# A sequence of four layers on one core: three edits to its last stage (who adds k's rotations, when GEGLU's tokens are transposed, and a drain written out step by step)

## The chip, the core and the metric

One core of a Trainium2 chip runs one program. Its engines work side by side, each through its own queue in order: TensorE (PE, with weight loads shown as PEld), VectorE (DVE), ScalarE (ACT), GpSimd (POOL) and SyncE (SP), which here only issues DMAs. The metric is the device time of one execution in microseconds (us); lower is better. For the kernel before, three runs took 1828.2, 1832.02 and 1840.76 us, a median of 1832.02.

## The reference, cut to what matters

The input is x, 8 batches of 512 tokens of 128 channels, float32. Four layers follow, each with a residual sum and a layer norm. Only the fourth is touched by the change; it is two rounds of local attention and a gated MLP:

```python
def _layer(x, wqkv, qs, ksc, wo, lg, lb, w1, b1, w2, b2):
    h = shift_token(x)                      # half of the channels come from the token before
    q, k, v = split(h @ wqkv)               # 8 heads of 64
    q = l2norm(q) * qs;  k = l2norm(k) * ksc
    q, k = rotary_xpos(q, k)                # q*cos + rotate_half(q)*sin, the same for k
    o = local_attention(q, k, v)            # windows of 64, each sees itself and the one before
    x = x + o @ wo
    h = layernorm(shift_token(x)) * lg + lb
    a, g = split(h @ w1 + b1)               # 341 columns each
    return x + (a * gelu(g)) @ w2 + b2
for l in range(2):
    x = _layer(x, wqkv[l], ...)
out = layernorm(x_in + x)
```

## The kernel before, in words

The four layers run one after the other. The fourth is `ffn1` (its loop is called the last stage here); its three first chunks are begun by `early`, inside the attention before it, and the rest is `main`. Work is cut into 16 *items* k (round l = k // 8, batch k % 8) of four *chunks* c of 128 tokens, 64 chunks in all (`LAST`). The loop at line 986 runs over steps t. Every step issues a bit of several chunks at different depths, in an order written out by hand, and every call is kept in program order (line 629), so that order is each engine's queue.

What step t issues, with c = t % 4, and the names the profile shows for it:

- `begin` (chunk t): the products `q_ps` and `k_ps`. `squares` (ACT) and `rotate` (DVE, lines 705 to 710) read them. `rotate` leaves two products for q (n = 0) and for k (n = 1): with the cosine in `r` (shown as `was_k`), with the sine in `t2` (shown as `was_q`).
- `sizes` (line 715): DVE reduces the squares by head (`was_v<-was_k`), POOL adds `t2` to `r` for q and k in one operation of 128x1024 (`was_k<-was_k,was_q`). `norms` (line 721), on POOL: a maximum, a power (`was_v<-was_v`, 128x16), and k times its reciprocal norm (`was_k<-was_k,was_v`, 128x512).
- `operands_T` (chunk t-1): PE transposes k's half of `r`, then q's (`t_ps`); ACT copies them (`kT`, `qT`).
- `scores`, `maxima`, `weights` (chunk t-2): PE puts the mask and the scores in `sp`; DVE takes maxima and scales them in `m<-m,was_v`; ACT makes eight exponentials `pw`. `over_sums` (t-3) divides them on POOL (`pw<-pw,den`). `weights_T`, `weights_taken`, `values`, `values_taken` (t-4): PE `p_ps`, DVE `pT`, PE `o_ps`, ACT `oT`.
- `sums` (t-5 for attention, t-11 for the MLP): PE `y_ps`, DVE adds to `xs`.
- Once per item, two items back: at c = 0, after `sums`, four DMAs load the shifted tokens `hn`. At c = 1 `normed` takes moments (DVE `bn`, `st`; POOL `rstd`, `mr`) and adds b2 and x to `xs` on POOL; ACT normalizes `hn` as the last thing but `sums`. At c = 2, after `maxima`, `geglu` (line 954) transposes `hn` (`nT`), ACT copies it, and three times PE makes `gp` and `ap`, ACT the Gelu `u`, DVE the product. In the second round a finished batch has its moments taken at c = 2 (`moments(.., "f")`), and at c = 3 `finished` (line 965) normalizes it on ACT (`xn`) and sends it out.

PSUM: `q_ps`, `k_ps` and the two `sp` tiles have one bank each; everything else takes turns in four banks (`bank`). The steps past t = `LAST` begin no chunk; they drain what is under way: the last four chunks' attention, the GEGLU of items 14 and 15, their sums, and the last three layer norms.

Of the kernel before, what the change touches and what calls it, by code (L numbers as in the profile page):

```python
# [9 lines left out]
F32 = mybir.dt.float32  # L10
# [3 lines left out]
AF = mybir.ActivationFunctionType  # L14
ALU = mybir.AluOpType
# [3 lines left out]
P = 128  # L19
B, S, D = 8, 512, 128  # L20
NT = S // P
# [13 lines left out]
HID = 341  # L35
H_CH = [(0, 128), (128, 128), (256, 85)]
# [15 lines left out]
def body(ctx, tc, x, consts, rows, wa0, wa1, acols, bo, wf, wqkv, wo, w1, w2, cols, b2r, qs, ks, out):  # L52
# [6 lines left out]
    xs = outer.tile([P, B * NT, D], F32, name="xs")  # L59
# [9 lines left out]
    w1_s = outer.tile([P, 2, 2 * HID], F32, name="w1_s")  # L69
    w2_s = outer.tile([P, 2, 3, D], F32, name="w2_s")  # L70
    cols_s = outer.tile([P, 2, 8], F32, name="cols_s")
# [11 lines left out]
    half = outer.tile([P, NT], F32, name="half")  # L83
    nc.vector.memset(half, -0.5)
    ident = cst[:, C_ID : C_ID + P]
# [539 lines left out]
    def ffn1():  # L625
# [4 lines left out]
        mm, tr, act, copy = kept(nc.tensor.matmul), kept(nc.tensor.transpose), kept(nc.scalar.activation), kept(nc.scalar.copy)  # L630
        v_tt, v_stt, v_max, v_copy = (
            kept(f) for f in (
                nc.vector.tensor_tensor, nc.vector.scalar_tensor_tensor, nc.vector.tensor_reduce, nc.vector.tensor_copy
            )
        )
        v_stats, v_aggr, v_inv = kept(nc.vector.bn_stats), kept(nc.vector.bn_aggr), kept(nc.vector.reciprocal)
        p_tt, p_ts, p_set = (
            kept(f) for f in (
                nc.gpsimd.tensor_tensor, nc.gpsimd.tensor_scalar, nc.gpsimd.memset
            )  # L640
        )
# [3 lines left out]
        PAD, K = 64, 2 * B  # L645
        LAST = NT * K
        item = [{} for _ in range(K)]
# [30 lines left out]
        def tables(l):  # L678
            for n in range(2):
                s = lambda a, z: sc[:, l, n, a:z].unsqueeze(1).broadcast_to([P, NT, z - a])  # L680
                for k, a, z, by in ((0, 0, 64, (0, 64)), (1, 0, 32, (32, 64)), (1, 32, 64, (0, 32))):
                    p_tt(tab[:, l, n, k, :, a:z], tab[:, l, n, k, :, a:z], s(*by), ALU.mult)

        def shifted(src, h):

            p_set(h[0:1, 0, 64:128], 0.0)
            for at, n in ((0, 112), (112, 15)):
                nc.sync.dma_start(out=h[at + 1 : at + 1 + n, :, 64:128], in_=src[at : at + n, :, 64:128])
            nc.sync.dma_start(out=h[0:1, 1:NT, 64:128], in_=src[P - 1 : P, 0 : NT - 1, 64:128])
            nc.sync.dma_start(out=h[:, :, 0:64], in_=src[:, :, 0:64])  # L690
            return h

        def rows_of(k):
            return slice((k % B) * NT, (k % B + 1) * NT)
# [20 lines left out]
        def sizes(k, c, h):  # L715
            ss = sss[(NT * k + c) % 2]
            v_max(ss, h.pop("sq").rearrange("p n (h d) -> p (n h) d", d=DH), AX.X, ALU.add)
            p_tt(h["r"], h["r"], h.pop("t2"), ALU.add)
            h["ss"] = ss

        def norms(k, c, h):
# [8 lines left out]
        def load(k):  # L730
            item[k]["h"] = shifted((xs if k >= B else xn)[:, rows_of(k), :], hq)
# [32 lines left out]
        def main():  # L764
            with ExitStack() as st:
# [3 lines left out]
                bank = lambda name: p_b.tile([P, S], F32, tag="b", name=name)  # L769
# [9 lines left out]
                for i in range(2):  # L779
                    t = const.tile([P, 4, PAD + S], F32, name=f"kT{i}")  # L780
                    nc.gpsimd.memset(t[:, :, 0:PAD], 0.0)
                    kTs.append(t)
                work = pool("w", 2)
# [14 lines left out]
                def transposed(src, name, bufs):  # L798
                    ps = bank(name)
                    for c in range(NT):  # L800
                        tr(ps[:, c * P : (c + 1) * P], src[:, c, :], ident)
                    t = work.tile([P, S], F32, tag=name, name=name, bufs=bufs)
                    copy(t, ps)
                    return t
# [137 lines left out]
                def normalized(x, dst, shape):  # L942
                    r, m = shape
                    for c in range(NT):
                        act(dst[:, c, :], x[:, c, :], AF.Identity, bias=m[:, c : c + 1], scale=r[:, c : c + 1])

                def normed(k):
                    l, x = k // B, xs[:, rows_of(k), :]
                    item[k]["shape"] = moments(item[k]["hn"], "h")
                    p_tt(x, x, b2[:, l, :].unsqueeze(1).broadcast_to([P, NT, D]), ALU.add)  # L950
                    if l:
                        p_tt(x, x, xn[:, rows_of(k), :], ALU.add)

                def geglu(k):
                    l, nT = k // B, transposed(item[k].pop("hn"), "nT", 1)
                    u = work.tile([P, 3, S], F32, tag="u", name="u", bufs=2)
                    for c, (at, n) in enumerate(H_CH):
                        gp, ap = bank("gp"), bank("ap")
                        for ps, o in ((gp, HID), (ap, 0)):
                            mm(ps[0:n], lhsT=w1_s[:, l, o + at : o + at + n], rhs=nT, start=True, stop=True)  # L960
                        act(u[0:n, c, :], gp[0:n], AF.Gelu, bias=cols_s[0:n, l, 3 + c : 4 + c])
                        v_stt(u[0:n, c, :], ap[0:n], cols_s[0:n, l, c : c + 1], u[0:n, c, :], ALU.add, ALU.mult)
                    item[k]["u"] = u

                def finished(b):
                    x = slice(b * NT, (b + 1) * NT)
                    normalized(xs[:, x, :], xn[:, x, :], item[B + b].pop("shape"))
                    nc.sync.dma_start(out=ov[:, b], in_=xn[:, x, :])
# [3 lines left out]
                def load_T(k):  # L972
                    item[k]["hT"] = transposed(item[k].pop("h"), "hT", 3)

                def at_(j, f, *a):
                    if 0 <= j < LAST:
                        f(*divmod(j, NT), chunk[j], *a)

                def begun(t, f, *a):
                    if t >= EARLY:  # L980
                        at_(t, f, *a)
# [1 line left out]
                def begin(k, c, h):  # L983
                    proj(k, c, h, [p_qk.tile([P, INNER], F32, tag=f"{n}", name=f"{n}_ps") for n in "qk"])

                for t in range(1, LAST + 11):
                    k, c = divmod(t, NT)
                    if c == 1 and k + 1 < K:
                        load(k + 1)
                    begun(t, begin)  # L990
                    at_(t - 4, weights_T)
                    begun(t, squares, 1)
                    begun(t, rotate, 0)
                    at_(t - 3, over_sums)
                    at_(t - 4, weights_taken)
                    at_(t - 2, scores)
                    begun(t, squares, 0)
                    at_(t - 2, maxima)
                    if c == 3 and k + 1 < K:
                        load_T(k + 1)  # L1000
                    if c == 2 and 0 <= k - 2 < K:
                        geglu(k - 2)
                    if c == 1 and 0 <= k - 2 < K:
                        normed(k - 2)
                    begun(t, rotate, 1)
                    at_(t - 2, v_of)
                    at_(t - 1, operands_T)
                    at_(t - 1, operands)
                    at_(t - 4, values)
                    begun(t, sizes)  # L1010
                    at_(t - 2, weights)
                    begun(t, norms)
                    at_(t - 4, values_taken)
                    if c == 1 and 0 <= k - 2 < K:
                        h = item[k - 2]["hn"]
                        normalized(h, h, item[k - 2].pop("shape"))
                    sums(t - 5, t - 11)
                    if c == 0 and 0 <= k - 2 < K:
                        hn = work.tile([P, NT, D], F32, tag="hn", name="hn", bufs=1)
                        item[k - 2]["hn"] = shifted(xs[:, rows_of(k - 2), :], hn)  # L1020
                    if t in (4, 5):
                        scaled_weights(t - 4)
                    if t == 6:
                        tables(1)
                    z = t - 11
                    if z >= B * NT and z % NT == NT - 1:
                        item[z // NT]["shape"] = moments(xs[:, rows_of(z // NT), :], "f")
                        if z == LAST - 1:
                            finished(B - 1)
                    if z > B * NT and z % NT == 0:  # L1030
                        finished(z // NT - 1 - B)

        return early, main

    with tc.tile_pool(name="ops", bufs=1) as ops:
# [50 lines left out]
        for i in range(2):  # L1086
            for j in range(2):
                nc.sync.dma_start(
                    out=ks_[i][64 * j + 32 : 64 * j + 48].bitcast(F32),
                    in_=rowq.bitcast(F32).unsqueeze(1).broadcast_to([16, 8, S]),  # L1090
                )
        last = ffn1()
        for _ in ffn0(qs_, ks_, va, second, lambda: attention(1, False, qs_, ks_, va, second, spare=last[0], alone=16)):
            pass
# [99 lines left out]
```

## Time and profile before

| | |
|---|---|
| median of three runs | 1832.02 us |
| the profiled execution | 1831.37 us, of which its span is 1829.6 us |
| busy over the span | PE 1652.3, DVE 1349.6, ACT 1257.1, POOL 945.1 us |
| last stage: `main` | from about 1087 us to the end |
| 1600 to 1700 us | PE 96.88, DVE 76.28, ACT 81.71, POOL 92.78 us, clock 1.00 |
| 1795 to 1802 us | PE 0.21 us, clock 0.69 |

The page gives the granted clock of PE as a share of full speed. In a timeline a row is: start, duration, engine, line, operation, what it writes <- what it reads, how often, and in square brackets the idle time of the engine before it and what ended that. Rows that follow each other closely are merged. All rows of the last stage have line 629, so operations are told apart by tile names.

### The profile page before, as it was taken

How to read it: one execution, taken by the hardware profiler on the slowest of the kernel's cores; microseconds unless marked ns; L12 is line 12 of the kernel's file. 1: busy time of each engine (PE TensorE's matmuls, PEld its weight loads, DVE VectorE, ACT ScalarE, POOL GpSimd, SP SyncE). 2: the span in 40 equal slices, each digit the busy share in tenths (PEclk: the TensorE clock that was granted, in tenths of full speed). 3: DMA queues.
4: the chain of work that ended last, by engine and by line, in shares of the span. 5: the costliest groups of instructions: out<-in, count | busy, mean ns of one | idle time of the engine just before them, and what ended most of it. 6: DMA issues, size and time to landing. Idle time of an engine off the chain costs nothing.

```text
span 1829.6 us, 41974 instructions
## 1 busy us (share of the span) xinstructions
PE 1652.3 (90%) x16292; PEld 952.5 (52%) x16293; DVE 1349.6 (74%) x2185; ACT 1257.1 (69%) x2992; POOL 945.1 (52%) x954
## 2 busy tenths in 40 slices
PE   1699999999977679999999988899999999999984
PEld 1345555455545544444444445566666666666653
DVE  2588778878848788888888947677777777777752
ACT  0277777777754437877778867777777777888872
POOL 3223322232124542323222268988888888999972
PEclk6699999999998889999999999999999999999997
DMA  6823222221110223332223101111111111111110
GB/s 114 210 65 69 57 52 60 55 65 25 14 13 1 49 61 79 71 70 54 60 64 60 42 1 36 30 38 39 35 33 38 34 37 35 42 39 39 33 33 24
DMA packets 92648, 90.25 MB, mean 49 GB/s; under 512 B 45937, under 2 KB 57969, under 8 KB 92450
## 3 DMA queue, kind: packets, MB, share of 16 engines
q1 hardware_dynamic: 87760, 86.57, 21.5%
q8 instruction: 129, 2.11, 0.5%
q0 software_dynamic: 4096, 0.54, 0.2%
q14 instruction: 69, 0.57, 0.1%
q10 hardware_dynamic: 594, 0.47, 0.1%
HBM read 41.85 MB, written 18.87 MB: 33 GB/s over the span
## 4 chain that ended last, share of the span: by engine, by line
PE 67%; POOL 12%; DVE 8%; ACT 7%; issue 2%; DMA 2%; SPq 1%; ACTq 0%; DVEq 0%; POOLq 0%
PE av L250 14%; PE s_ps L250 11%; PE t_ps L250 9%; POOL was_k L629 4%; POOL was_v L629 4%; PE y_ps L629 4%; PE sp L629 3%; PE gp L629 2%; PE o_ps L629 2%; ACT e L48 2%; PE ap L629 2%; PE o_ps L251 2%; PE t_ps L629 2%; PE q_ps L629 2%; PE k_ps L629 2%
## 5 line engine op out<-in xcount | busy, mean ns | idle before, releaser
L48 DVE TENSOR_REDUCE m<-s_ps 128x2 f32<-128x1024 f32 x512 | 621.4, 1224 | 171.4 <-PE s_ps L250 167.3
L48 ACT ACTIVATE e<-t_ps 128x512 f32<-128x512 f32 x1024 | 556.2, 596 | 183.5 <-PE t_ps L250 175.9
L250 PE MATMUL av<-e,va 128*32 128x256 f32 x4096 | 328.5, 393 | 10.8 <-ACT avs L48 10.7
L250 PE MATMUL s_ps<-k,q 63*128 63x512 f32 x1024 | 264.2, 511 | 31.7 <-DMA k<-far 23.0
L48 POOL DMA_DIRECT2D q<-mt x128 | 69.1, 543 | 368.8 <-ACT mt L48 368.7
L250 PE MATMUL t_ps<-q,k 64*128 64x512 f32 x1024 | 247.1, 447 | 1.3 <-ACT e L48 1.3
L629 ACT ACTIVATE pw<-sp,m,was_v 128x128 f32<-128x128 f32 x512 | 227.3, 475 | 0.9
L250 PEld LDWEIGHTS s_ps<-k,q 63*128 63x128 f32 x1024 | 99.1, 189 | 238.8 <-issue 160.0
L629 POOL TENSOR_TENSOR was_v<-was_v 128x16 f32<-128x16 f32 x64 | 187.7, 2933 | 5.3
L629 POOL TENSOR_TENSOR was_k<-was_k,was_q 128x1024 f32<-128x1024 f32 x64 | 151.1, 2361 | 61.8 <-DVE was_q L629 61.7
L250 PEld LDWEIGHTS av<-e,va 128*32 128x32 f32 x4096 | 81.8, 108 | 101.1 <-issue 59.2
L250 PEld LDWEIGHTS t_ps<-q,k 64*128 64x128 f32 x1024 | 122.0, 189 | 22.6 <-ACT e L48 10.6
L629 POOL TENSOR_TENSOR pw<-pw,den 128x1024 f32<-128x1024 f32 x64 | 121.3, 1896 | 7.6 <-DVE den L629 7.6
L629 ACT ACTIVATION_READ_ACCUMULATOR pw<-sp,m,was_v 128x1 f32 x512 | 113.3, 221 | 0.0
L250 PEld LDWEIGHTS <-sel 64*128 64x128 bf16 x2048 | 66.7, 97 | 75.8 <-issue 43.5
L629 DVE TENSOR_REDUCE m<-sp 128x4 f32<-128x512 f32 x128 | 82.5, 686 | 27.7 <-PE sp L629 25.8
L629 ACT COPY v<-v_ps 128x512 f32<-128x512 f32 x64 | 37.5, 586 | 83.0 <-PE v_ps L629 83.0
L629 PEld LDWEIGHTS t_ps<-cst,was_k 128*128 128x128 f32 x512 | 57.7, 141 | 60.8 <-POOL was_k L629 42.8
L48 POOL CAST parts<-x 128x512 fp32r<-128x512 f32 x32 | 19.5, 609 | 132.9 <-ACT x L48 132.9
L629 DVE SCALAR_TENSOR_TENSOR u<-ap,cols_s,u 128x512 f32<-128x512 f32 (+1 forms) x48 | 36.0, 749 | 69.3 <-PE ap L629 69.3
L629 PE MATMUL t_ps<-cst,was_k 128*128 128x128 f32 x512 | 67.7, 275 | 20.6 <-POOL was_k L629 19.7
L629 DVE COPY pT<-p_ps 128x512 f32<-128x512 f32 x128 | 80.4, 670 | 0.0
(190 smaller groups left out, 3261.3 us busy)
## 6 DMA issues: line engine op xcount, KB each, us to landing
far<-parts SPq DMA_DIRECT2D x64, 256.0 KB
q<-far SPq DMA_DIRECT2D x256, 64.0 KB
k<-far SPq DMA_DIRECT2D x256, 64.0 KB
ve<-v SPq DMA_DIRECT2D x112, 128.0 KB
xn<-in_x SPq DMA_DIRECT2D x8, 256.0 KB
q<-mt POOLq DMA_DIRECT2D x128, 4.0 KB, 3.0
hn<-xs SPq DMA_DIRECT2D x16, 128.0 KB
out<-xn SPq DMA_DIRECT2D x8, 256.0 KB
```

What stands on the lines that cost most here:

```text
L48: return lambda *a, **k: self.tc.keep_in_program_order(f(*a, **k))
L250: mm = lambda *a, **k: tc.keep_in_program_order(nc.tensor.matmul(*a, **k))
L251: tr = lambda *a, **k: tc.keep_in_program_order(nc.tensor.transpose(*a, **k))
L629: kept = lambda f: lambda *a, **k: tc.keep_in_program_order(f(*a, **k))
```

## The change

`sizes`: DVE adds k's half (128x512) right after its reduction, POOL only q's half (128x512). `geglu` is split in `turned` (four transposes), `turned_taken` (ACT's copy) and `gated` (one of three column groups, whole or for one half of the tokens). In the loop `turned` is issued at c = 2 ahead of `squares` and so ahead of `scores`; `turned_taken` stands between the two `squares`. The loop ends at `LAST` - 1, and the rest is written out: item 14's MLP now comes after the last attention chunks, item 15's by halves of its tokens, each half followed by its sums; the three last layer norms are placed by hand (`ended`). What is computed stays the same.

```diff
--- before.py
+++ after.py
@@ -715,7 +715,8 @@
         def sizes(k, c, h):
             ss = sss[(NT * k + c) % 2]
             v_max(ss, h.pop("sq").rearrange("p n (h d) -> p (n h) d", d=DH), AX.X, ALU.add)
-            p_tt(h["r"], h["r"], h.pop("t2"), ALU.add)
+            v_tt(h["r"][:, 1], h["r"][:, 1], h["t2"][:, 1], ALU.add)
+            p_tt(h["r"][:, 0], h["r"][:, 0], h.pop("t2")[:, 0], ALU.add)
             h["ss"] = ss
         def norms(k, c, h):
@@ -951,16 +952,28 @@
                     if l:
                         p_tt(x, x, xn[:, rows_of(k), :], ALU.add)
+                def turned(k):
+                    item[k]["nT_ps"], hn = bank("nT"), item[k].pop("hn")
+                    for c in range(NT):
+                        tr(item[k]["nT_ps"][:, c * P : (c + 1) * P], hn[:, c, :], ident)
+                def turned_taken(k):
+                    item[k]["nT"] = work.tile([P, S], F32, tag="nT", name="nT", bufs=1)
+                    copy(item[k]["nT"], item[k].pop("nT_ps"))
                 def geglu(k):
-                    l, nT = k // B, transposed(item[k].pop("hn"), "nT", 1)
-                    u = work.tile([P, 3, S], F32, tag="u", name="u", bufs=2)
-                    for c, (at, n) in enumerate(H_CH):
-                        gp, ap = bank("gp"), bank("ap")
-                        for ps, o in ((gp, HID), (ap, 0)):
-                            mm(ps[0:n], lhsT=w1_s[:, l, o + at : o + at + n], rhs=nT, start=True, stop=True)
-                        act(u[0:n, c, :], gp[0:n], AF.Gelu, bias=cols_s[0:n, l, 3 + c : 4 + c])
-                        v_stt(u[0:n, c, :], ap[0:n], cols_s[0:n, l, c : c + 1], u[0:n, c, :], ALU.add, ALU.mult)
-                    item[k]["u"] = u
+                    item[k]["u"] = work.tile([P, 3, S], F32, tag="u", name="u", bufs=2)
+                    for c in range(3):
+                        gated(k, c)
+                def gated(k, c, half=None):
+                    l, nT, u, (at, n) = k // B, item[k]["nT"], item[k]["u"], H_CH[c]
+                    to = slice(0, S) if half is None else slice(half * S // 2, (half + 1) * S // 2)
+                    gp, ap = bank("gp")[0:n, to], bank("ap")[0:n, to]
+                    for ps, o in ((gp, HID), (ap, 0)):
+                        mm(ps, lhsT=w1_s[:, l, o + at : o + at + n], rhs=nT[:, to], start=True, stop=True)
+                    act(u[0:n, c, to], gp, AF.Gelu, bias=cols_s[0:n, l, 3 + c : 4 + c])
+                    v_stt(u[0:n, c, to], ap, cols_s[0:n, l, c : c + 1], u[0:n, c, to], ALU.add, ALU.mult)
                 def finished(b):
                     x = slice(b * NT, (b + 1) * NT)
@@ -983,13 +996,17 @@
                 def begin(k, c, h):
                     proj(k, c, h, [p_qk.tile([P, INNER], F32, tag=f"{n}", name=f"{n}_ps") for n in "qk"])
-                for t in range(1, LAST + 11):
+                for t in range(1, LAST):
                     k, c = divmod(t, NT)
                     if c == 1 and k + 1 < K:
                         load(k + 1)
                     begun(t, begin)
                     at_(t - 4, weights_T)
+                    if c == 2 and 0 <= k - 2 < K:
+                        turned(k - 2)
                     begun(t, squares, 1)
+                    if c == 2 and 0 <= k - 2 < K:
+                        turned_taken(k - 2)
                     begun(t, rotate, 0)
                     at_(t - 3, over_sums)
                     at_(t - 4, weights_taken)
@@ -1025,10 +1042,72 @@
                     z = t - 11
                     if z >= B * NT and z % NT == NT - 1:
                         item[z // NT]["shape"] = moments(xs[:, rows_of(z // NT), :], "f")
-                        if z == LAST - 1:
-                            finished(B - 1)
                     if z > B * NT and z % NT == 0:
                         finished(z // NT - 1 - B)
+                def rest(t):
+                    at_(t - 4, weights_T)
+                    at_(t - 3, over_sums)
+                    at_(t - 4, weights_taken)
+                    at_(t - 2, scores)
+                    at_(t - 2, maxima)
+                    at_(t - 2, v_of)
+                    at_(t - 1, operands_T)
+                    at_(t - 1, operands)
+                    at_(t - 4, values)
+                    at_(t - 2, weights)
+                    at_(t - 4, values_taken)
+                def begin_hn(k):
+                    hn = work.tile([P, NT, D], F32, tag="hn", name="hn", bufs=1)
+                    item[k]["hn"] = shifted(xs[:, rows_of(k), :], hn)
+                def scaled(k):
+                    h = item[k]["hn"]
+                    normalized(h, h, item[k].pop("shape"))
+                def ended(k):
+                    item[k]["shape"] = moments(xs[:, rows_of(k), :], "f")
+                    finished(k - B)
+                E, L = K - 2, K - 1
+                rest(LAST)
+                sums(LAST - 5, LAST - 11)
+                begin_hn(E)
+                rest(LAST + 1)
+                normed(E)
+                scaled(E)
+                sums(LAST - 4, LAST - 10)
+                rest(LAST + 2)
+                sums(LAST - 3, LAST - 9)
+                turned(E)
+                turned_taken(E)
+                rest(LAST + 3)
+                sums(LAST - 2, LAST)
+                sums(LAST - 1, LAST)
+                begin_hn(L)
+                item[E]["u"] = work.tile([P, 3, S], F32, tag="u", name="u", bufs=2)
+                gated(E, 0)
+                gated(E, 1)
+                normed(L)
+                gated(E, 2)
+                scaled(L)
+                ended(E - 1)
+                for z in range(4):
+                    sums(LAST, LAST - 8 + z)
+                turned(L)
+                turned_taken(L)
+                item[L]["u"] = work.tile([P, 3, S], F32, tag="u", name="u", bufs=2)
+                for n in range(2):
+                    for c in range(3):
+                        gated(L, c, n)
+                    if n == 0:
+                        ended(E)
+                    for z in range(2):
+                        sums(LAST, LAST - 4 + 2 * n + z)
+                ended(L)
         return early, main
```

## The prediction

> **What bounds it now.** Read first: the busy shares by stretch. From 1600 to 1700 us PE is busy 96.88 us, POOL 92.78. So PE sets the pace of the last stage and only what makes PE wait can be won. The table of waits says what that is (who waited for whom: total, times, longest; two lines for 1200 to 1560 us, where round 0 runs, two for 1560 to 1735 us, round 1):
>
> ```profile
> PE t_ps L629 <- POOL was_k L629: 9.0, 9, 1.0
> PE gp L629 <- ACT nT L629: 5.4, 8, 0.7
> ```
>
> ```profile
> PE gp L629 <- ACT nT L629: 2.7, 4, 0.7
> PE t_ps L629 <- POOL was_k L629: 2.2, 4, 0.6
> ```
>
> Two waits per item, one for each of the first two edits. The timelines of POOL, of PE and of DVE show the first, and a second effect:
>
> ```profile
> 1414.67 1.90 POOL L629 TENSOR_TENSOR pw<-pw,den 128x1024 f32<-128x1024 f32 x1
> 1417.94 2.36 POOL L629 TENSOR_TENSOR was_k<-was_k,was_q 128x1024 f32<-128x1024 f32 x1 [1.37 <-DVE was_q L629]
> 1420.26 0.26 POOL L629 TENSOR_SCALAR was_v<-was_v 128x16 f32<-128x16 f32 x1
> 1420.60 2.93 POOL L629 TENSOR_TENSOR was_v<-was_v 128x16 f32<-128x16 f32 x1
> 1423.61 1.04 POOL L629 TENSOR_TENSOR was_k<-was_k,was_v 128x512 f32<-128x512 f32 x1
> ```
>
> ```profile
> 1422.58 1.12 PE L629 MATMUL v_ps<-wqkv_s,hT 128*128 128x512 f32 x2
> 1424.71 1.09 PE L629 MATMUL t_ps<-cst,was_k 128*128 128x128 f32 x8 [1.00 <-POOL was_k L629]
> ```
>
> ```profile
> 1415.34 1.25 DVE L629 SCALAR_TENSOR_TENSOR m<-m,was_v 128x8 f32<-128x8 f32 x1
> ...
> 1434.06 0.17 DVE L629 SCALAR_TENSOR_TENSOR m<-m,was_v 128x8 f32<-128x8 f32 x1
> ```
>
> POOL's sum, power and product stand between DVE's rotations and PE's transposes. DVE's tiny `m`, with two inputs in SBUF, takes 0.17 us inside a power (POOL's runs from 1432.68 to 1435.61), but 1.25 while POOL's `pw` runs: it ends as `pw` ends (1416.59 and 1416.57).
>
> The second wait, at c = 2, on PE and then on ACT:
>
> ```profile
> 1689.40 1.04 PE L629 MATMUL p_ps<-cst,pw 128*128 128x128 f32 x8
> 1690.27 0.59 PE L629 MATMUL sp<-mask,identb 128*128 128x512 bf16 x2
> 1690.80 1.10 PE L629 MATMUL sp<-kT,qT 64*64 64x128 f32 x32
> 1691.83 0.66 PE L629 MATMUL nT<-cst,hn 128*128 128x128 f32 x4
> 1693.17 1.12 PE L629 MATMUL gp<-nT,w_s 128*128 128x512 f32 x2 [0.68 <-ACT nT L629]
> ```
>
> ```profile
> 1689.70 1.68 ACT L629 ACTIVATE hn<-hn,mr,rstd 128x128 f32<-128x128 f32 x4
> ```
>
> **k's rotations on DVE.** POOL's sum shrinks from 2.36 to about half (1.18, the same operation at half its size; the 128x512 sum into `xs` takes 1.27), and needs only q's rotation, done long before. The chain now runs: DVE's reduction (1.20), DVE's sum, POOL's maximum (0.25 and 0.08 to the next), power 2.93, product 1.04. DVE's sum has no row; 128x512 rotations with one input in PSUM start every 0.60 us, so 0.60, which is also half of the 128x1024 reduction; the upper bound is 0.98, four 128x128 sums into `xs` at 0.49 the pair. POOL's maximum reads SBUF too and may wait for it; I let it wait. The product's new wait, for DVE's sum, ends 3 us before the power does. From the rotations' end that gives 1.14 + 0.60 + 0.33 + 3.01 + 1.10 = 6.18 to `t_ps` against 6.99 before (1417.72 to 1424.71). Besides, the same chain one step earlier ends sooner: DVE's reduction there ends at 1408.98, its sum at 1409.5, and 0.33, 3.01 and 1.00 later `pw` starts at 1413.84 (before 1414.67) and ends at 1415.74. So `m` is released 0.85 sooner, and the rotations begin that much earlier. Sum: `t_ps` could start 1.66 earlier; PE needs 1.27, as `v_ps` begins at 1422.58 and the next product follows 0.86 behind (1423.44). So the wait goes.
>
> What it is worth per item, from starts: in round 0, 1.27 at c = 1 and 0.10 at c = 0 (1414.80 against 1413.84 + 0.86); in round 1, 0.80 (`v_ps` 1673.53, `t_ps` 1675.19) and 0.10. So 43.44 - 1.37 = 42.07 and 42.96 - 0.90 = 42.06: both rounds fall to one period, that of PE with only the second wait left. 9 x 1.37 + 4 x 0.90 = **15.9 us**.
>
> On DVE the sum adds 64 x 0.60 = 38 us in idle time: 23.7 us of 100 were idle, 10.2 per item, and it takes 2.4. Queued behind it are the sums into `xs`, which waited 1.64, 1.27 and 1.44 us for PE at c = 0, 3 and 2. At c = 1 there is no such slack, and POOL's `xs` sum (1.28) may hold it too: rotations and `pT` come about 1 us later, and the next thing late is the maximum of `sp`, which the second edit delays anyway.
>
> At the start POOL alone was the chain (PE waits of 1.37, 0.31, 1.62 and 3.18 us at 1123, 1133, 1143 and 1154). The first k there: rotations from 1114.93 as before, reduction to 1117.33, sum to 1117.9, then 0.33, 3.01 and 1.04: 1122.3. From one k to the next POOL has a scaling `w_s` (1.28), `pw` (1.88), q's sum (1.2), DVE's sum in a gap (0.6) and again 4.4: 1131.6. A memset (0.5) more gives 1141.5; the tables (`was_q`, 3.04) in place of `w_s` and DVE's sum, by then done, give 1152.0. PE gets to the last three at 1131.7, 1140.2 and 1149.6 (9.3, 8.5 and 8.1 us from one `t_ps` to the next, waits taken off). So 1152.0 replaces 1154.88: **2.8** (4.1 if the maximum does not wait four times). At 1091.79 PE waits 0.88 for POOL's memset of `kT` behind the third early chunk; that chunk's chain (reduction to 1085.62) ends 0.5 sooner: **0.5**.
>
> **`nT` ahead of the scores.** The scores then hide ACT's copy, and `gp` no longer waits. But `hn` is the tail of ACT's queue of that step (1689.70 + 1.68 = 1691.38), and PE reaches the new place at 1690.27. The last transpose starts at 1691.43, the mask about 0.2 later, then mask 0.53 and scores 1.03: `gp` at 1693.2, against 1693.17. ACT's queue starts from `v_ps` like PE's path, so removing the first wait moves both. The wait changes its name, from `gp` <- `nT` to `nT` <- `hn`: **0**, with 0.85 per item as the one bound and -0.6 (if PE's restart costs as much as ACT's copy) as the other.
>
> **The drain.** Its end before, on ACT:
>
> ```profile
> 1801.24 1.65 ACT L629 ACTIVATE hn<-hn,mr,rstd 128x128 f32<-128x128 f32 x4 [8.88 <-POOL mr L629]
> 1803.46 0.59 ACT L629 COPY nT<-nT 128x512 f32<-128x512 f32 x1 [0.56 <-PE nT L629]
> ```
>
> On this trace's clock: the last `t_ps` at 1759.4 (k by the chain above) in place of 1761.15. Everything keeps that 1.75 until 1770; so ACT's last exponentials end at 1771.3 and POOL's two `xs` sums of item 14 at 1774.3. Item 14's GEGLU (1776.2 to 1783.3) leaves the path: the last two chunks' values come at 1772.9 (after DVE's `pT`, 1.24 behind its reciprocal at 1771.5) and at 1778.4 (POOL's last `pw` 1774.3 to 1776.2, `p_ps` 0.97, `pT` 1.2). Then `o_ps` 1.08, ACT's copy 0.6, four products: the last attention sum stands in `xs` at 1781.8 instead of 1794.0. SP has nothing else queued there, so the four DMAs take the 4.0 of before (1794.0 to `bn` at 1798.03): `bn` 1785.8, `hn` 1789.0, with item 14's GEGLU under them. That is 12.2 ahead.
>
> Then ACT's queue gives much of it back. Ahead of `nT`'s copy stands the layer norm of batch 5: its `mr` comes on POOL after the two `xs` sums (2.6) and four small operations (1.97), at 1793.5; four `xn` take 1.65; the copy ends at 1795.7 and `gp` starts at 1795.75, only 8.3 ahead. PE has idled over 4 us and restarts slowly: before, after such a pause, `gp` and `ap` took 1.7 to 1.9 in place of 0.86 until 1807.7, clock 0.51 from 1802 to 1808. The first half has six products of 0.43, 2.58 us; 3.7 us at half speed do 1.85 of it, so it ends at 1800.2, DVE's last `u` at 1800.95. In the second half ACT's Gelus stand behind batch 6's `xn` (`bn` 1800.95, `mr` 1804.15, `xn` to 1805.8): Gelus from 1805.8, `u` to 1808.0, sums in `xs` to 1809.2, `bn` to `xn` 3.3 as before (1815.04 to 1818.31), last `xn` at 1812.4, before at 1818.31, and the 11.3 behind it stay: **5.9 us**, 1.75 of them the wait at 1761.
>
> Sum: 0.5 + 2.8 + 15.9 + 0 + 5.9 = 25.1; 1831.4 - 25.1 = 1806, the median lying 0.65 above the profiled run: **1807 us**.
>
> **Rivals.** (a) The reorder pays in full: 13 x 0.85 = 11 more, 1796. `hn`'s row speaks against it. Chance 0.10.
>
> (b) The port takes the wait's place. If DVE's sum waits for POOL's sum of q (1.18) as `m` did for `pw`, k comes 1.2 later where 0.4 is to spare: 9 x 0.8 + 2.8 lost, 1817. It decides from 0.4 us of mean hold. Against: that sum of POOL's ends before DVE's reduction in the steps that decide. Chance 0.17.
>
> (c) Slower: DVE becomes the bound. If POOL's maximum and power go first and the power holds DVE's sum, each step blocks DVE 0.33 + 2.93 us. DVE's item is then 32.8 + 2.4 + 13.0 = 48.2, against 43.3 on the mean now: 13 x 4.9 - 9 = 55 slower, 1887. It decides from 1.7 us of hold per step ((42.07 - 35.2) / 4). The rows for it are `m` at 1.25, the row against it `m` at 0.17 inside a power. Chance 0.09.
> By the Trainium skill, SBUF — State Buffer, section "Who interferes with whom", a DVE instruction with two SBUF inputs contends with a GpSimd one that reads SBUF, and whoever issues first holds the port for the whole instruction. By that rule the power would hold DVE as in (c); the trace agrees for `pw` (1.25) and not for the power (0.17).
>
> **Numbers.** Forecast 0.64, (a) 0.10, (b) 0.17, (c) 0.09. The forecast's own bounds: the start +1.3, the reorder -0.6 x 13 = -8, the drain -4 (if ACT's order costs nothing) to +4. Range **1796 to 1818**: it takes in (a) and (b). A measurement tells about 1% (18 us) from no change: faster than that 0.75 (forecast, (a) and a sliver of (b)), within it 0.16 ((b)), slower 0.09 ((c)).
>
> **What would show it.** No PE wait for `was_k` after 1200 us and periods of 42.1 between `gp` starts; `nT` <- `hn` near 0.8 per item; `t_ps` near 1152 in the start; `xn` of batch 5 ahead of `nT`'s copy. Wrong if the periods stay near 43, or DVE's sum takes far over 0.6.

## The result, and the profile after

| kernel | median of runs | lowest to highest | ratio to before (95%) |
|---|---|---|---|
| before | 1832.76 us | 1828.2 to 1840.76, 4 runs | |
| changed | 1811.68 us | 1809.44 to 1815.7, 4 runs | 0.9883 [0.9843, 0.9922] |

The profiled execution took 1810.46 us (span 1808.6), 20.9 less than the 1831.37 of before. Cut at the first `gp` of each item, and at the first `t_ps` of the last stage (1091.79 before, 1089.78 after), that is:

| stretch | before | after | gain | forecast |
|---|---|---|---|---|
| ahead of the last stage | 1091.79 | 1089.78 | 2.0 | 0.5 |
| its start, to the first `gp` | 81.55 | 76.34 | 5.2 | 2.8 |
| round 0, 9 items | 390.95 (43.44 each) | 380.27 (42.25) | 10.7 | 12.3 |
| round 1, 4 items | 171.85 (42.96) | 172.16 (43.04) | -0.3 | 3.6 |
| drain, to the end of the span | 93.46 | 90.05 | 3.4 | 5.9 |

The waits of PE in the changed kernel, from 1200 to 1546 us (round 0) and from 1546 to 1719 us (round 1); who waited for whom, then total, times, longest. The two names of before are gone, one new one is there in each round:

```profile
PE nT L629 <- ACT hn L629: 6.3, 9, 0.7
```

```profile
PE nT L629 <- ACT hn L629: 3.4, 4, 0.9
```

The first edit's chain in round 0, on POOL's timeline of the changed kernel (q's sum, maximum, power, k's product):

```profile
1424.94 1.26 POOL L629 TENSOR_TENSOR was_k<-was_k,was_q 128x512 f32<-128x512 f32 x1
1428.32 0.62 POOL L629 TENSOR_SCALAR was_v<-was_v 128x16 f32<-128x16 f32 x1 [2.12 <-DVE was_v L629]
1429.03 2.93 POOL L629 TENSOR_TENSOR was_v<-was_v 128x16 f32<-128x16 f32 x1
1432.03 1.04 POOL L629 TENSOR_TENSOR was_k<-was_k,was_v 128x512 f32<-128x512 f32 x1
```

and on DVE's, in the same step:

```profile
1428.15 0.68 DVE L629 TENSOR_TENSOR was_k<-was_k,was_q 128x512 f32<-128x512 f32 x1
```

The sum that took POOL 2.36 us is now 1.26 there and 0.68 on DVE. POOL's maximum, 0.26 us before, began inside DVE's sum and took 0.62: it ended 0.1 us behind the sum, as the forecast had allowed. At c = 1 the sum itself is held, once per item, in both rounds (1.58 to 1.67 us). There it begins while POOL adds to `xs`, and POOL's next instruction is stretched in turn; POOL's rows, then DVE's:

```profile
1372.99 1.27 POOL L629 TENSOR_TENSOR xs<-xs,was_v 128x512 f32<-128x512 f32 x1
1374.22 1.73 POOL L629 TENSOR_TENSOR was_k<-was_k,was_q 128x512 f32<-128x512 f32 x1
```

```profile
1373.23 1.58 DVE L629 TENSOR_TENSOR was_k<-was_k,was_q 128x512 f32<-128x512 f32 x1
```

On PE the second edit reads:

```profile
1415.82 1.04 PE L629 MATMUL p_ps<-cst,pw 128*128 128x128 f32 x8
1417.56 0.69 PE L629 MATMUL nT<-cst,hn 128*128 128x128 f32 x4 [0.70 <-ACT hn L629]
1418.08 0.60 PE L629 MATMUL sp<-mask,identb 128*128 128x512 bf16 x2
1418.61 1.10 PE L629 MATMUL sp<-kT,qT 64*64 64x128 f32 x32
1419.64 1.13 PE L629 MATMUL gp<-nT,w_s 128*128 128x512 f32 x2
```

`gp` no longer waits, `nT` waits 0.70 for `hn`. Round 1 got nothing, and the waits do not say why: PE's `v_ps` is followed by `t_ps` not 0.86 us behind its start but 1.24, as k's product ends (1655.91 + 1.04).

```profile
1655.77 1.12 PE L629 MATMUL v_ps<-wqkv_s,hT 128*128 128x512 f32 x2
1657.01 1.09 PE L629 MATMUL t_ps<-cst,was_k 128*128 128x128 f32 x8
```

DVE's `m` shows what changed there; its instructions in round 1, before and after (nanoseconds, shortest, median and longest):

```profile
L629 DVE SCALAR_TENSOR_TENSOR m<-m,was_v x16: 166/186/1210, 1564.4 to 1727.5; 128x8 f32<-128x8 f32 x16
```

```profile
L629 DVE SCALAR_TENSOR_TENSOR m<-m,was_v x16: 166/1592/1729, 1547.9 to 1709.4; 128x8 f32<-128x8 f32 x16
```

The median went from 0.19 to 1.59 us. The two timelines of the changed kernel show how, POOL's first and then DVE's:

```profile
1647.87 1.90 POOL L629 TENSOR_TENSOR pw<-pw,den 128x1024 f32<-128x1024 f32 x1
...
1652.20 0.62 POOL L629 TENSOR_SCALAR was_v<-was_v 128x16 f32<-128x16 f32 x1 [1.20 <-DVE was_v L629]
...
1656.91 1.90 POOL L629 TENSOR_TENSOR pw<-pw,den 128x1024 f32<-128x1024 f32 x1
```

```profile
1648.17 1.62 DVE L629 SCALAR_TENSOR_TENSOR m<-m,was_v 128x8 f32<-128x8 f32 x1
...
1652.04 0.68 DVE L629 TENSOR_TENSOR was_k<-was_k,was_q 128x512 f32<-128x512 f32 x1
...
1657.28 1.55 DVE L629 SCALAR_TENSOR_TENSOR m<-m,was_v 128x8 f32<-128x8 f32 x1
```

Each `pw` starts 0.3 us ahead of an `m`, which then ends with it (1648.17 + 1.62 = 1649.79; 1647.87 + 1.90 = 1649.77). Before, `pw` started just behind `m` in those steps; POOL's rows of the kernel before, then DVE's:

```profile
1666.46 1.90 POOL L629 TENSOR_TENSOR pw<-pw,den 128x1024 f32<-128x1024 f32 x1
...
1675.10 1.90 POOL L629 TENSOR_TENSOR pw<-pw,den 128x1024 f32<-128x1024 f32 x1
```

```profile
1665.92 0.17 DVE L629 SCALAR_TENSOR_TENSOR m<-m,was_v 128x8 f32<-128x8 f32 x1
...
1675.03 0.17 DVE L629 SCALAR_TENSOR_TENSOR m<-m,was_v 128x8 f32<-128x8 f32 x1
```

This reads as a ring: `pw` holds `m`, `m` delays k's rotations and the reduction, DVE's sum holds POOL's maximum, then power and product, then the next `pw`: 1656.91 - 1647.87 = 9.04 us round, while PE's step from `q_ps` to `q_ps` is 8.72 where it waits for nothing (1599.07 to 1607.79 in moments_behind_pw, below).

In the drain ACT's queue was the price, as worked out: four `xn` ahead of `nT`'s copy, and PE waits.

```profile
1777.51 1.65 ACT L629 ACTIVATE xn<-xs,mr,rstd 128x128 f32<-128x128 f32 x4 [2.96 <-POOL mr L629]
1779.06 0.56 ACT L629 COPY nT<-nT 128x512 f32<-128x512 f32 x1
```

```profile
1779.67 1.22 PE L629 MATMUL gp<-nT,w_s 128*128 128x256 f32 x2 [4.74 <-ACT nT L629]
...
1790.92 0.66 PE L629 MATMUL gp<-nT,w_s 128*85 128x256 f32 x2 [2.23 <-ACT u L629]
```

### The profile page after: what moved, and what is told of

The parts are those of the page before. It is cut to its first block, busy times and chain, and to the rows that moved or that the text cites. A ratio compares the mean times of both kernels' runs of the same rounds, so it can differ in the third digit from the quotient of the medians.

```text
span 1808.6 us, 42091 instructions
## 1 busy us (share of the span) xinstructions
PE 1647.8 (91%) x16305; PEld 954.6 (53%) x16305; DVE 1415.4 (78%) x2252; ACT 1256.4 (69%) x2995; POOL 898.6 (50%) x954
## 4 chain that ended last, share of the span: by engine, by line
PE 69%; DVE 11%; ACT 7%; POOL 5%; DMA 3%; issue 3%; SPq 1%; ACTq 0%; DVEq 0%; POOLq 0%
PE av L250 15%; PE s_ps L250 12%; PE t_ps L250 9%; PE sp L629 4%; PE y_ps L629 4%; PE gp L629 2%; PE o_ps L629 2%; ACT e L48 2%; PE ap L629 2%; PE o_ps L251 2%; PE t_ps L629 2%; DVE m L629 2%; PE v_ps L629 2%; PE p_ps L629 2%; PE q_ps L629 2%
## 5 line engine op out<-in xcount | busy, mean ns | idle before, releaser
L250 PE MATMUL av<-e,va 128*32 128x256 f32 x4096 | 328.6, 393 | 10.8 <-ACT avs L48 10.7
L629 POOL TENSOR_TENSOR was_k<-was_k,was_q 128x512 f32<-128x512 f32 x64 | 85.5, 1336 | 6.1 <-DVE was_q L629 6.1
L629 DVE TENSOR_REDUCE was_v<-was_k 128x16 f32<-128x1024 f32 x64 | 77.0, 1203 | 0.0
L629 PEld LDWEIGHTS p_ps<-cst,pw 128*128 128x128 f32 x512 | 59.7, 141 | 32.6 <-issue 25.6
```

The lines of the kernel that those rows point to most:

```text
L250: mm = lambda *a, **k: tc.keep_in_program_order(nc.tensor.matmul(*a, **k))
L629: kept = lambda f: lambda *a, **k: tc.keep_in_program_order(f(*a, **k))
```

## The experiments

Whole times of two profiles differ by up to 12 us in what lies ahead of the last stage: its first `t_ps` comes at 1087.3 to 1099.4 us in kernels that differ there by next to nothing, and at 1087.3, 1091.8 and 1098.5 in three that have the same code up to there. (The 1103.0 of one expectation is no run's first `t_ps`.) So each run is read by its stretches:

| run | median us | ratio to before (95%) | round 0, per item | round 1, per item | drain |
|---|---|---|---|---|---|
| k_sum_only | 1822.16 | 0.9945 [0.9926, 0.9963] | 42.48 | 43.30 | 94.1 |
| turned_first_only | 1831.33 | 1.0000 [0.9977, 1.0023] | 43.25 | 42.90 | 94.6 |
| drain_only | 1830.05 | 0.9987 [0.9968, 1.0006] | 43.43 | 42.94 | 92.1 |
| no_turned_first | 1819.14 | 0.9918 [0.9893, 0.9944] | 42.48 | 43.33 | 90.2 |
| sum_after_xs | 1811.11 | 0.9866 [0.9843, 0.9889] | 42.07 | 42.07 | 90.9 |
| m_from_psum | 1811.27 | 0.9874 [0.9852, 0.9895] | 42.07 | 42.07 | 91.0 |
| turned_behind_scores | 1802.14 | 0.9821 [0.9793, 0.9848] | 41.29 | 42.27 | 88.0 |
| drain_in_act_order | 1813.80 | 0.9882 [0.9860, 0.9904] | 42.26 | 43.05 | 85.1 |
| all_three_moves | 1798.12 | 0.9822 [0.9802, 0.9842] | 41.38 | 42.22 | 84.6 |
| changed_again | 1813.79 | 0.9902 [0.9880, 0.9923] | 42.26 | 43.06 | 91.3 |
| moments_behind_pw | 1791.30 | 0.9789 [0.9758, 0.9819] | 41.38 | 41.29 | 84.0 |
| three_moves_m_psum | 1791.53 | 0.9799 [0.9770, 0.9829] | 41.29 | 41.28 | 83.3 |

### The parts alone

**k_sum_only**: of the change, only this.

```
-            p_tt(h["r"], h["r"], h.pop("t2"), ALU.add)
+            v_tt(h["r"][:, 1], h["r"][:, 1], h["t2"][:, 1], ALU.add)
+            p_tt(h["r"][:, 0], h["r"][:, 0], h.pop("t2")[:, 0], ALU.add)
```

> The kernel before with the first part of the change alone: DVE sums k's rotations, POOL q's; GEGLU's tokens are transposed where they were, and the drain is the old one. My theory (all of the gain up to the drain is POOL's wait for k's sum; the transposes gain and lose nothing; in round 1 a hold of m by POOL's pw eats what the k sum gives): first gp at 1166 to 1168 us as in the changed kernel, period of an item in round 0 42.25 +-0.15, in round 1 43.0 +-0.15, drain as before (93.5), in all about 15 us under the kernel before, 1815 to 1818. Rival 1 (the transposes ahead of the scores are what eats round 1's gain): period in round 1 42.1 here, in all 1812. Rival 2 (the start's surplus of two microseconds comes with the transposes): first gp at 1168 to 1170.

The sum wins 0.96 per item in round 0 and loses 0.34 in round 1 (43.30 against 42.96): the new ring is its work alone, so rival 1 falls. But 42.48 and 43.30 are not the changed kernel's 42.25 and 43.04, and the whole is 4 to 7 us over what I expected: the transposes are not worth nothing. PE waits here 0.95 us for `nT`'s copy, where it was 0.68. Rival 2 falls too: from the first `t_ps` to the first `gp` no_turned_first, below, takes 76.28 us without the second edit, the changed kernel 76.34 with it (the 77.82 of k_sum_only hold a slow clock of PE, see the last section).

**turned_first_only**: of the change, only the calls of `turned` and `turned_taken` behind `weights_T` and `squares`.

> The kernel before with the second part alone: GEGLU's tokens transposed ahead of the scores. My theory (the wait only changes its name, PE's wait for nT's copy, 0.8 us, becomes a wait for hn): 1831 +-2, round 0 43.4 +-0.2 and round 1 43.0 +-0.2 per item; at c=2 PE waits 0.7 to 0.9 us ahead of nT and not ahead of gp. Rival (it pays 0.8 us on each of 13 items, being covered while POOL is the bound): 1821. Second rival (it costs, since the wait now stands ahead of the scores): up to 1841.

Nothing in all. While POOL sets the pace, 0.19 per item come back in round 0 and 0.06 in round 1. No wait stands in front of `nT`, but its four transposes take 1.32 us instead of 0.66 (1437.18 to 1438.50), while ACT makes the four parts of `hn` (1436.42 to 1438.12): by these times each waits for its part. A wait can sit inside a group's time.

**drain_only**: of the change, only the functions from `rest` on and the calls behind them.

> The kernel before with the third part alone: the drain of its own. My theory: everything up to the last loop step as before, and the drain, from the last gp of the loop to the end, 3 to 4 us shorter than the 93.46 of before: 1828 us. Rival (the drain's shorter time in the changed kernel came with the k sum on DVE, whose wait at the first t_ps of the drain is 1.0 us shorter there): 1829.5.

The drain gains 1.3 us (93.46 to 92.1), less than either theory; beside the sum on DVE it gains 3.9 (94.1 to 90.2 below). The 2.6 between them are two things. With POOL's sum of 2.36 the first `t_ps` still waits 2.00 us, where the changed kernel waits 1.05. And behind that wait the clock was 0.64 over 4.7 us, so that PE came from `t_ps` to the second `y_ps` in 4.61 us (1755.32 to 1759.93) instead of 3.10; this looks like chance, since the kernel before kept 1.00 there after 2.03 us. Without that the gain would be about 2.8, an estimate from these rows.

**no_turned_first**: the changed kernel with

```
-                    if c == 2 and 0 <= k - 2 < K:
-                        turned(k - 2)
                     begun(t, squares, 1)
-                    if c == 2 and 0 <= k - 2 < K:
-                        turned_taken(k - 2)
...
                     if c == 2 and 0 <= k - 2 < K:
+                        turned(k - 2)
+                        turned_taken(k - 2)
                         geglu(k - 2)
```

> The changed kernel without its second part: the transposes of GEGLU's tokens again right ahead of GEGLU. My theory (second part worth nothing): 1811 +-1.5, round 0 42.25, round 1 43.0, PE waiting 0.8 us for nT's copy at each c=2 in the place of 0.7 to 0.9 for hn. Rival (the second part delays the chain in round 1 by its wait): round 1 42.1, 1808. Other rival (second part is worth its 0.8 per item): 1821.

Between my theory and the second rival: once POOL's wait is gone, the transposes ahead of the scores are worth 0.23 per item in round 0 and 0.29 in round 1, because the wait they trade away has grown to 0.95 and 1.2 (at 1463.94 in this run ACT's squares of q, ahead of the copy in its queue, have waited 0.39 for DVE's rotation). 9 x 0.23 + 4 x 0.29 = 3.2 us; the medians differ by 5.4 and 7.5, of which the traces show no more than that.

### The ring, opened at two places

**sum_after_xs**: `norms` follows the sum.

```
-            v_tt(h["r"][:, 1], h["r"][:, 1], h["t2"][:, 1], ALU.add)
...
+        def summed(k, c, h):
+            v_tt(h["r"][:, 1], h["r"][:, 1], h.pop("t2")[:, 1], ALU.add)
...
-                    begun(t, norms)
                     at_(t - 4, values_taken)
...
                     sums(t - 5, t - 11)
+                    begun(t, summed)
+                    begun(t, norms)
```

> The changed kernel with DVE's sum of k's rotations moved from right behind the reduction to behind the step's two additions into xs (and POOL's maximum, power and product asked for after it), so that the sum no longer holds POOL's maximum (0.62 us where it is 0.25). My theory (round 1 runs at the pace of a ring: POOL's pw holds m, m delays the rotations and the reduction, the sum holds POOL's maximum, the power and the product set the next pw, 9.04 us round where PE's step is 8.71): the maximum back at 0.25, the ring 8.5 to 8.7, round 1 from 43.04 to 42.2-42.5 per item, round 0 unchanged at 42.25; 1808 to 1810 in all. Rival (m is held in any case and the t_ps wait of round 1 comes from DVE's own load): round 1 stays at 43.0. Rival on the other side (the sum now comes after y_ps and delays POOL's product by a microsecond): round 0 rises to 43 or more, 1820.

**m_from_psum**:

```
-                    v_stt(m, m, -1.0, h["nq"], ALU.mult, ALU.mult)
+                    v_stt(m, h["sp"][1][:, 0, 0:8].rearrange("p (s r) -> p s r", s=2), 0.0, h["nq"], ALU.mult, ALU.mult)
```

> The changed kernel with one operand of m's product read from the score's PSUM tile, times 0, in the place of m in SBUF; so the maxima are computed and not used, and the exponents are taken without them. Only one SBUF operand is left to that instruction. My theory (an instruction of DVE with two SBUF operands waits while POOL's pw or q sum holds SBUF, one with a PSUM operand does not): m 0.17 to 0.2 us at every step where it is 0.8 to 1.7 now, round 1 from 43.04 to 42.2-42.5 per item, round 0 unchanged. Rival (m's 1.6 us is something else, such as waiting for nq from POOL's power): m stays long and round 1 at 43.0. Rival 2 (m becomes short, but round 1 is set elsewhere): m 0.2 and 43.0.

Both give 42.07 in both rounds, what the forecast had for them (42.07 and 42.06; the last digits by luck, since the reorder's 0.23 was not in it), by opening the ring at different places: one takes the hold off POOL's maximum, the other the hold off `m`. In sum_after_xs `m` is still held at three of four steps of round 1 (0.82 to 1.05 us), at no cost. So the ring is shown, and it also cost round 0 its 0.18 per item, which I had not expected. POOL's timeline of sum_after_xs, then DVE's:

```profile
1656.30 0.25 POOL L629 TENSOR_SCALAR was_v<-was_v 128x16 f32<-128x16 f32 x1 [1.20 <-DVE was_v L629]
1656.63 2.93 POOL L629 TENSOR_TENSOR was_v<-was_v 128x16 f32<-128x16 f32 x1
```

```profile
1656.80 0.68 DVE L629 TENSOR_TENSOR was_k<-was_k,was_q 128x512 f32<-128x512 f32 x1
```

The maximum is back at 0.25, and the sum, now inside a power, takes 0.68 as ever. And `m` in m_from_psum, from 1175 to 1722 us:

```profile
L629 DVE SCALAR_TENSOR_TENSOR m<-sp,was_v x52: 165/167/168, 1176.9 to 1713.8; 128x8 f32<-128x8 f32 x52
```

Fifty-two times 0.17 us, with `pw` running or not. By the Trainium skill, SBUF — State Buffer, section "Who interferes with whom", a DVE instruction with at most one SBUF input, outside the modes that use both of its port pairs, does not contend with GpSimd, and one with two contends with a GpSimd instruction that reads SBUF. The trace agrees for `pw` and `m` with both halves of that. In whole time the two runs hardly stand out from the changed kernel: their profiles entered the last stage 6 to 10 us later.

### The other two waits

**turned_behind_scores**: `turned` behind `scores`, `turned_taken` behind the squares there, and

```
+                    if c == 2:
+                        at_(t - 2, v_of)
                     if c == 2 and 0 <= k - 2 < K:
                         geglu(k - 2)
...
-                    at_(t - 2, v_of)
+                    if c != 2:
+                        at_(t - 2, v_of)
```

> The changed kernel with GEGLU's tokens transposed behind the scores, and v's projection of that step put between them and GEGLU, so that both the wait for hn (0.70 in round 0, 0.92 in round 1) and the wait for nT's copy (0.95 and 1.2 without the second part of the change) have work of PE in front. My theory (PE is the bound of round 0, and of round 1 at c=2): 0.6 to 0.7 less per item in round 0 (41.55 to 41.65), about as much in round 1, 1803 to 1805 in all. Rival (the freed time turns into waits of t_ps for POOL's and DVE's chain): period stays above 42.1 in round 0.

More than expected: 0.96 per item in round 0 and 0.77 in round 1. The scores cover `hn`, `v_ps` covers the copy, and PE shows no wait in the item from 1503 to 1544 us, so 41.29 is PE's own time for an item. Round 1 keeps 42.27: the ring is still there (`m` 1.44 and 1.73 us at two steps of an item).

**drain_in_act_order**:

```
-                ended(E - 1)
-                for z in range(4):
-                    sums(LAST, LAST - 8 + z)
                 turned(L)
                 turned_taken(L)
+                ended(E - 1)
+                for z in range(4):
+                    sums(LAST, LAST - 8 + z)
...
-                    if n == 0:
+                    if n:
                         ended(E)
```

> The changed kernel with two moves in its drain: the last GEGLU's tokens are transposed and copied ahead of the normalization of the output before the last but one, and the normalization of the last but one waits until the last GEGLU's second half has been asked for. My theory (ACT's queue is what PE waits for there: 4.74 us for nT's copy and 2.23 for u): the two waits fall to about 1 and 0.3, and the end gets 4 to 6 us earlier, 1805 to 1808, with nothing changed up to the drain. Rival (what is moved back lies on the last chain, since ACT and the output's transfer end later): gain under 2 us. Second rival (hn, not the queue, is late: its transfer ends only then): nT's wait keeps 3 us or more under the name of hn.

The drain gains 5.0 us against the first profile of the changed kernel and 6.2 against the second (90.05 and 91.3 to 85.1), as my theory had it, though the second rival is right about the name: 3.15 us remain, for `hn`. The whole time does not show the gain, with 9 us more ahead of the stage. PE's timeline:

```profile
1782.81 1.48 PE L629 MATMUL nT<-cst,hn 128*128 128x128 f32 x4 [3.15 <-ACT hn L629]
1784.13 4.47 PE L629 MATMUL y_ps<-w_s,u 128*128 128x128 f32 x24
1788.44 0.60 PE L629 MATMUL gp<-nT,w_s 128*128 128x256 f32 x2
```

The sums now stand behind that wait and take 4.47 us at a clock of 0.60, where they took 3.1 in the changed kernel (there it was the first half's `gp` and `ap`, 1.06 to 1.22 a pair, that ran slowly; here they take 0.59 to 0.60).

### Together

> The changed kernel with the three moves that the runs so far support: DVE's sum behind the additions into xs, the transposes behind the scores with v's projection between them and GEGLU, and the drain in the other order of ACT. My theory (each removes another wait, so they add): round 0 41.2 to 41.3 per item, no better than with the transposes alone (PE's own work is all that is left there), round 1 41.2 to 41.4 (the sum takes away the ring that kept it at 42.27 with the transposes alone), drain 83 to 85.5 where it was 90.05; from the first gp to the end about 621 us where it was 642.5, in all some 21 us under the changed kernel, 1789 to 1793. Rival (with less wait on PE the ring closes again at the shorter step): round 1 41.8 or more, 1793 to 1796.

> The changed kernel itself beside the one above on the same chip, since whole times of two profiles differ by up to 13 us in what lies ahead of the last stage (its first t_ps at 1089.8 to 1103.0 in runs whose code is the same up to there). By all theories: round 0 42.25, round 1 43.04, drain 90 to 91, and 0.988 of the kernel before.

Side by side: 1798.12 against 1813.79, 15.7 us instead of some 21. The drain came as expected, and round 0 in eight of its nine items (41.29; the first took 42.12). Round 1 did not: 42.22, the rival's number. PE's, POOL's and DVE's timelines of all_three_moves:

```profile
1608.10 1.09 PE L629 MATMUL t_ps<-cst,was_k 128*128 128x128 f32 x8 [0.72 <-POOL was_k L629]
```

```profile
1598.75 0.20 POOL L629 TENSOR_TENSOR mr<-st,rstd 128x4 f32<-128x4 f32 x1
1598.90 1.90 POOL L629 TENSOR_TENSOR pw<-pw,den 128x1024 f32<-128x1024 f32 x1
```

```profile
1598.92 1.90 DVE L629 SCALAR_TENSOR_TENSOR m<-m,was_v 128x8 f32<-128x8 f32 x1
```

It is not the ring but one step of it: the output's moments (1597.01 to 1598.95) put `pw` off to 0.02 us ahead of `m`, which is held for all of it. Two more runs ask whether it is that hold or POOL's load.

**moments_behind_pw**: the POOL part of `moments` is a function `shape_of`, called a step later.

```
-                        item[z // NT]["shape"] = moments(xs[:, rows_of(z // NT), :], "f")
+                        item[z // NT]["st"] = moments(xs[:, rows_of(z // NT), :], "f", False)
...
+                    late = t - 12
+                    if late >= B * NT and late % NT == NT - 1:
+                        item[late // NT]["shape"] = shape_of(item[late // NT].pop("st"), "f")
                     sums(t - 5, t - 11)
```

> The kernel of the three moves, with POOL's four instructions of the output's moments (1.9 us in all, round 1 only, now ahead of POOL's pw of c=0) put behind pw and q's sum of that step, where POOL then idles. My theory (in the kernel of the three moves they start pw 1.9 us late, just ahead of DVE's m, which is held for the whole of pw, 1.90 us; that makes the k product late and PE waits 0.72 us for it at the next t_ps): m at that step 0.17 to 0.9, no 0.72 wait, round 1 from 42.22 to 41.3-41.6 per item, round 0 and drain unchanged, 2.5 to 3.5 us less in all. Rival (PE's wait follows from POOL's own load at c=0, which stays the same): round 1 42.0 to 42.3.

**three_moves_m_psum**: all_three_moves with the edit of m_from_psum.

> The kernel of the three moves with one operand of m's product from PSUM, times 0 (the maxima are computed and not used). My theory (the hold of m is what is left of round 1): m 0.17 throughout, round 1 41.3 to 41.6 per item. Rival (POOL's own load at c=0 sets it): 42.0 to 42.3, with PE's wait of 0.7 at the t_ps after c=0 as before.

Both reach PE's own time in round 1 (41.29 and 41.28), with no wait of PE between 1585 and 1700 us: the hold it was, since POOL's load in three_moves_m_psum is that of all_three_moves. In moments_behind_pw the hold is shorter, not gone: `m` at that step takes 1.12 us, more than expected, behind q's sum, as `pw` had ended before. moments_behind_pw computes everything and is as fast as any run, 1791.3 us, 20.4 and 22.5 under the two measurements of the changed kernel. Its profile is 6.6 us under that of all_three_moves: 3.7 of them are round 1's, 1.8 the start's, where PE's clock happened to be 1.00 here and 0.63 there.

## Why the prediction came out as it did

The sign was right, and the time within its range: 1811.68 against 1807. The sum forecast 25.1 and the profiles show 20.9, but part of that is luck: 2.0 lie ahead of the last stage, where profiles of the same code differ by more, and 1.1 in a clock that the second profile of the changed kernel did not get. From the first `t_ps` to the end the forecast was 24.6; the two profiles of the changed kernel show 19.0 and 16.5.

- **Round 0, 1.37 per item forecast, 1.19 measured.** Mechanism right: no `t_ps` wait, and a period of 42.07 as soon as the ring is open. The costs of DVE's sum (0.60 from start to start), POOL's half (1.26 for 1.18) and the waiting maximum (0.62) were right. So was the fear for c = 1, where POOL's `xs` sum holds DVE's sum (1.58); PE waits only for `hn` in the steps around it.
- **Round 1, 0.90 forecast, -0.08 measured.** The step that failed: "So `m` is released 0.85 sooner, and the rotations begin that much earlier" (0.83 by its own figures, 1414.67 to 1413.84). That holds where `pw` already ran ahead of `m`. In two steps of round 1 `pw` had stood 0.07 and 0.54 us behind `m`; 0.85 sooner puts it ahead, and what had not been held is held. The working followed one step, c = 1, of one item. By the prediction's own sign ("Wrong if the periods stay near 43") this half of it was wrong. Opening the ring brought 5.5 us over both rounds (9 x 0.18 + 4 x 0.97).
- **The reorder, 0 forecast.** The wait changed its name as told (0.70 to 0.92), and alone it gave nothing. Beside the first edit it is worth about 3.2 us, since ACT's copy waits longer once POOL's wait is gone.
- **The start, 2.8 forecast, 5.2 measured** (4.0 by the second profile). Mis-sized in its first link, "rotations from 1114.93 as before": they began at 1111.72, which is 1113.73 on the clock of before, since the `pw` ahead of them came 1.2 us sooner and held `m` for 0.28 us where it was 1.15. The chain kept that 1.2. Another 1.1 us came from PE's clock, below, by chance. The early chunks' 0.5 did not come: PE waits 0.88 us at the first `t_ps` in both.
- **The drain, 5.9 forecast, 3.4 measured** (2.2 by the second profile). ACT's order and both waits came as worked out. 1.3 us are k's chain again (`t_ps` 1760.7 on the clock of before, not 1759.4). 1.0 is the first half of the last GEGLU: its six products took 0.85 to 1.02 us each from start to start, twice the 0.43 of the second half, all the way, where the forecast took 3.7 us at half speed.
- **The rivals.** (b) named the resource, and in the loop not the place: there q's sum did not hold DVE's sum, `pw` held `m`. Only at the start it did as (b) says, twice (1.45 and 1.82 us). (c) did not come: neither `m` nor DVE's sum was held inside a power. (a) was out of reach by putting `nT` there, though the 0.85 per item was there to have: turned_behind_scores won more.

## What to carry to other kernels

Where two engines share a resource that the first to start keeps, an instruction that gets earlier can overtake the one that it used to follow: list the starts of both in every step of the period, not in one. A wait is covered only by work that stands between the producer and the consumer, so between two dependent hops through another engine (here `hn` to `nT` to `gp`) put one piece of independent work in each gap. When whole times differ by more than the effect, compare the stretches between markers, and the granted clock in each.

## What the runs showed of the hardware

PE's clock after a wait. The changed kernel and k_sum_only both waited 2.08 us at the last slow `t_ps` of the start; the next 4.6 us follow (length; busy us and instructions of PE, PEld, DVE, ACT and POOL; granted clock, DMA share, GB/s), changed kernel first, and last the second profile of the changed kernel, after the same 2.08 us:

```profile
1148.79:1153.40 4.61, 4.61 (x52) 3.59 (x53) 3.08 (x4) 3.91 (x15) 4.53 (x4) 1.00 0.20 48
```

```profile
1154.54:1159.20 4.66, 4.66 (x49) 4.38 (x50) 2.35 (x2) 3.96 (x16) 4.58 (x4) 0.63 0.21 47
```

```profile
1152.90:1157.50 4.60, 4.60 (x48) 4.20 (x49) 2.35 (x2) 3.19 (x12) 4.52 (x4) 0.63 0.21 48
```

After the same wait the clock was 1.00 in one profile of the changed kernel and 0.63 in the other; the kernel before, after 3.18 us, had 0.63 as well. By the Trainium skill, TensorE: Matmul & The Clock Gate, section "Part 1: The HAM clock gate (the "warmup" mystery)", the window that decides runs free of the kernel, so the same gap may or may not fall into it; the traces agree with that chance. That section counts an idle window of about 3.4 us, and here 2.08 us of waiting were enough. After the drain's 4.74 us the clock was 0.58 on the mean over 7.1 us (1779.67 to 1786.80) in which PE never paused.

POOL's power reads SBUF, and yet `m` (0.17) and a 128x512 sum (0.68) ran inside it unheld. Once it began inside DVE's sum, at 1603.57 in all_three_moves, and took 3.36 instead of 2.93: it seems to wait for the other at its start and not to hold it later. No run measured that by itself.
